# Row counts over pairs of columns, and ranks counted from 1024, in the dilation beside an attention

## The chip, the cores and the metric

The kernel runs on one core of a Trainium2 chip. The time is the device time of one execution in microseconds (us), as the median of several runs; lower is better. The engines are PE (TensorE, matrix products; its weight loads are listed as PEld), DVE (VectorE), ACT (ScalarE), POOL (GpSimd) and SP (SyncE, here a queue of DMAs). Each works through its own instructions in order, and they wait for one another by semaphores.

## What is computed

There are B = 16 graphs of N = 1024 nodes with D = 128 features, and an adjacency `adj` of floats, zero where there is no edge. Layer 0 is an attention with 8 heads over the edges, layer 1 a "dilation" of the adjacency and three SAGE layers on what it leaves:

```python
# layer 0
scores = q @ k.T / sqrt(HD); scores[adj == 0] = -inf
attn = softmax(scores) * adj;  attn = attn / (attn.sum(-1) + 1e-8);  x = x + (attn @ v) @ Wo.T + bo
# layer 1: dilation, row by row
def step(carry, n):
    row = carry[n]
    num = sum(row)
    sf = where(num > 10, (num + 1) // 2, 1)
    rank = cumsum(row)
    rm = row & (rank % sf == 0)          # only if mask[n] and num > 1
    carry[n] = row & ~rm
    carry[:, n] = carry[:, n] & ~rm      # later rows see the removal
# then three times: relu(normalise((adj_d @ h / deg) @ Wr + h @ Wx + b)), batch norm; a last product
```

The dilation needs the running count (rank) of every row's edges. A row with more than 10 edges loses the edges of rank sf and 2 sf.

## The kernel before

All instructions of PE, ACT and DVE stand in an order written out by hand: each engine executes in the order in which the Python code emits.

**Attention** (`attention`, L472 to L613). A *turn* is one graph b, one half c of the query nodes (512) and one of 8 blocks m of 128 key nodes; there are 256 turns. Each has two *half-steps*, g = 0 and 1, with four heads each: 512 half-steps. In a half-step PE writes the mask and the scores of the *next* half-step into PSUM (`scores`, L546 and L552), later the products with the values (`values`, L479 with v1 as the weights, L484 with the small eps8); ACT takes two exponentials of 128 x 1024 (L590); DVE multiplies both by the adjacency (L595). In half-step g = 0 PE also transposes a block of the adjacency (L497), and ACT copies it (L500) and makes the mask from it (L504). The preparation of the next graph (`prepare`: layer norm, projections to q, k, v) and the conclusion of the last one (`conclude`) are spread over the half-steps. `v1` holds the values of a graph, for each key block m and head h 16 columns of values, a column of ones (whose product gives the sum), and zeros up to 32; two such buffers take turns in one tile.

**Dilation** (`dilation`, L643 to L934) is a generator that `beside_attention` (L936) advances between the half-steps. It goes over 8 blocks k of 128 rows, all 16 graphs b together. Each block has two parts, called *stages* below:

- *Block stage*: the 128 x 128 diagonal block of each graph. `up` is the upper triangle of the edges (L741), `w` the running count in it by two scans (L747), restarted for each graph by a zero in `go_on`. The transposed edges (PE, L763) give `valid` (L779, L782); L785 makes of w the count plus 1024 where valid and 0 elsewhere. Seven rounds then find the removed edges: small instructions compute the rank that each row removes (L805 to L828), L830 compares w with it, and PE sums what is hit (L836 to L841). At the end (L845 to L858) the numbers needed for whole rows are formed: `mid_at`, `off` and `allof`.
- *Column stage*: the whole rows, graph after graph. For graph b, a scan on DVE (L893) counts along the 1024 columns; it adds the column before and the column itself, so that each value is the sum of two neighbouring counts. ACT takes the distance to the middle, |value - 3 num| by an Abs with a bias per row (L906). DVE compares it with `off` (L910: one comparison catches both ranks), and masks with the edges (L913, L915). PE transposes the result (L900), ACT copies it (L902), and DMAs write both to DRAM (L923 to L927). ACT then reads the rows of the next block as signs (L691, L695), and `survive` (L708) takes the edges out that earlier blocks removed.

`rk(b, lo, hi)` is a slice of the resident edges of the current 128 rows of graph b, as bf16 zeros and ones; columns 0 and 1 are zeros and the edges begin at column 2.

**The order.** Each `yield cost, when` of the dilation says what the coming work costs (in us, by hand) and in which half-step it may run: `when` 0 is at once, 1 the next half-step, "A" an even one (g = 0), "B" an odd one. The loop in `beside_attention` lets the dilation go on while `spent` is below a straight line from 0 to `total`, with 16 half-steps of lead. The steps with a scan yield "B" and those with the comparison yield "A", so that a graph takes two half-steps.

**After that** three SAGE layers run (L1204 on), bound to PE and DMAs; nothing of them is touched.

Of the kernel before, what the change touches and what calls it, by code (L numbers as in the profile page):

```python
# [10 lines left out]
F32 = mybir.dt.float32  # L11
BF = mybir.dt.bfloat16
F16 = mybir.dt.float16
U8 = mybir.dt.uint8
I32 = mybir.dt.int32
AF = mybir.ActivationFunctionType
ALU = mybir.AluOpType
# [4 lines left out]
P = 128  # L22
# [4 lines left out]
ROUNDS = 7  # L27
# [7 lines left out]
def swept(ctx: ExitStack, tc: tile.TileContext, t: dict, out: bass.AP, flag: bass.AP):  # L35
# [8 lines left out]
    nc = tc.nc  # L44
    x, adj, nodemask = t["x"], t["adj"], t["nodemask"]
    B, N, D = x.shape
    H = 8
    HD = D // H
    NB = N // P
    HB = NB // 2  # L50
    HN = N // 2
# [115 lines left out]
    def first_part(p1):  # L167
# [71 lines left out]
            )  # L239


        v1_both = shared.tile([P, 2, NB, H, 32], F32, name="v1_both", tag="aT2")
        v1s = [v1_both[:, i] for i in range(2)]
        for v1 in v1s:
            nc.vector.memset(v1[:, :, :, HD:], 0.0)
            nc.vector.memset(v1[:, :, :, HD : HD + 1], 1.0)
        never = one.tile([P, P], BF, name="never")
        nc.vector.tensor_scalar(never, ident, -BIG, None, ALU.mult)

# [35 lines left out]
        def prepare(b):  # L285


            yield False
            xt = xts.pop(b)
            h = shared.tile([P, NB, D], F32, name=f"h_{b}", tag="s", bufs=2)  # L290
            hT = shared.tile([P, N], F32, name=f"hT_{b}", tag="s", bufs=2)

            def turned(c, bank=(ps_m, "m")):
                pt = bank[0].tile([P, 512], F32, name=f"pt_{b}_{c}", tag=bank[1])
                for i in range(HB):
                    nc.tensor.transpose(pt[:, i * P : (i + 1) * P], h[:, c * HB + i, :], ident)
                yield "evict"
                nc.scalar.copy(hT[:, c * HN : (c + 1) * HN], pt[:, :HN])


            kT = pool.tile([P, N], F32, name=f"kT_{b}", tag="kT")

            def query(c, bank=(ps_m, "m")):
                pq = bank[0].tile([P, 512], F32, name=f"pq_{b}_{c}", tag=bank[1])
                nc.tensor.matmul(pq, wts["Wq"], hT[:, c * HN : (c + 1) * HN], start=True, stop=True)
                yield "evict"
                for g in range(2):
                    nc.scalar.activation(  # L308
                        qTs[c][:, g, :], pq, AF.Identity, bias=bq[:, g : g + 1], scale=own[:, g : g + 1]
                    )  # L310

            def key(c, bank=(ps_m, "m")):
                cc = slice(c * HN, (c + 1) * HN)
                pk = bank[0].tile([P, 512], F32, name=f"pk_{b}_{c}", tag=bank[1])
                nc.tensor.matmul(pk, wts["Wk"], hT[:, cc], start=True, stop=True)
                yield "evict"
                nc.scalar.activation(kT[:, cc], pk, AF.Identity, bias=bk)

            v1 = v1s[b % 2]

            def value(c, bank=(ps_m, "m")):
                pv = bank[0].tile([P, HB, D], F32, name=f"pv_{b}_{c}", tag=bank[1])
                start_with(pv, 0)
                for i in range(HB):
                    n = (c * HB + i) * P
                    nc.tensor.matmul(
                        pv[:, i, :], hT[:, n : n + P], wts["Wv"], start=False, stop=(i == HB - 1)
                    )
                yield "evict"
                nc.scalar.copy(  # L330
                    v1[:, c * HB : (c + 1) * HB, :, :HD], pv.rearrange("p k (h d) -> p k h d", d=HD)
                )

            if b == 0:

                first = layer_norm_relu(h, xt, "a0", 0, HB)
                for _ in range(2):
                    next(first)
                yield "weights"
                yield from first  # L340
                yield "weights"
                yield "biases"
                yield from turned(0)
                yield "turn 1"
                second = layer_norm_relu(h, xt, "a0", HB, NB)
                for _ in range(2):
                    next(second)
                yield from key(0)
                qTs = [pool.tile([P, 2, HN], F32, name=f"qT_{b}_0", tag="qT")]
                yield from query(0, (ps_d, "d"))  # L350
                yield from second
                ready[b] = (xt, qTs, kT, v1)
                yield True
                yield from value(0, (ps_d, "d"))
                yield True
                yield from turned(1)
            else:
                yield from layer_norm_relu(h, xt, f"a{b}")
                for c in range(2):
                    yield True  # L360
                    yield from turned(c)
                for what in (key, value):
                    yield True
                    yield from what(0)

                yield "half 1"
                qTs = [pool.tile([P, 2, HN], F32, name=f"qT_{b}_0", tag="qT")]
                yield True
                yield from query(0)

            ready[b] = (xt, qTs, kT, v1)
            for what in (key, value):
                yield True
                yield from what(1)
            yield "half 0"
            qTs.append(pool.tile([P, 2, HN], F32, name=f"qT_{b}_1", tag="qT"))
            yield True
            yield from query(1)
# [93 lines left out]
        def attention():  # L472
# [3 lines left out]
            def values(acc, v1, m, g, es, ws):  # L476

                for j in range(4):
                    nc.tensor.matmul(  # L479
                        acc[g][32 * j : 32 * j + 32, :], v1[:, m, 2 * j + g, :],  # L480
                        ws[j // 2][:, j % 2, :], start=(m == 0), stop=False,
                    )
                for j in range(4):
                    nc.tensor.matmul(  # L484
                        acc[g][32 * j : 32 * j + 32, :], eps8,
                        es[j // 2][:, j % 2, :], start=False, stop=(m == NB - 1),
                    )
# [141 lines left out]
        def each_half(ap):  # L629
            return ap.unsqueeze(1).to_broadcast([P, B // 2, P])  # L630
# [12 lines left out]
        def dilation():  # L643
# [9 lines left out]
            def rk(b, lo, hi):  # L653
                return rks[b // (B // 2)][:, b % (B // 2), lo:hi]
# [73 lines left out]
            for k in range(NB):  # L728
# [3 lines left out]
                dgs = [rks[i][:, :, 2 + n0 : 2 + n1] for i in range(2)]  # L732
                halves = [slice(0, B // 2), slice(B // 2, B)]

                up = shared.tile([P, B, P], BF, name=f"up_{k}", tag="mr", bufs=4)

                go_on = shared.tile([P, B, P], BF, name=f"go_on_{k}", tag="mr", bufs=4)
                nc.gpsimd.memset(go_on, 1.0)
                nc.gpsimd.memset(go_on[:, :, 0:1], 0.0)
                for dg, hb in zip(dgs, halves):  # L740
                    nc.vector.tensor_tensor(up[:, hb, :], dg, each_half(upto), ALU.mult)  # L741
                next(late, None)
                yield 1.3, 1
                w = shared.tile([P, B, P], F16, name=f"w_{k}", tag="mr", bufs=4)
# [15 lines left out]
                for c, hb in enumerate(halves):  # L760
# [1 line left out]
                    for b in range(B // 2):  # L762
                        nc.tensor.transpose(pd[:, b, :], dgs[c][:, b, :], ident_bf)  # L763
                    if c == 0:
                        nc.vector.tensor_copy(onw, w[:, :, P - 1])
                        for dg, of in zip(dgs, halves):
                            nc.vector.tensor_reduce(last1[:, of], dg, AX.X, ALU.add)
                    else:
# [13 lines left out]
                nc.vector.tensor_tensor(valid, valid, each(beyond), ALU.mult)  # L782
                yield 1.2, 1

                nc.vector.scalar_tensor_tensor(  # L785
                    w.rearrange("p b i -> p (b i)"), w.rearrange("p b i -> p (b i)"), 1024.0,
                    valid.rearrange("p b i -> p (b i)"), ALU.add, ALU.mult,
                )
                yield 2.3, 1
                final = shared.tile([P, B, P], BF, name=f"final_{k}", tag="mr", bufs=4)  # L790
                nc.vector.tensor_tensor(in_pairs(final), in_pairs(w), over_rows(end16), ALU.is_equal)
                yield 1.3, 1
# [49 lines left out]

                th = small.tile([P, 4, B], F32, name=f"th_{k}", tag="th", bufs=2)  # L845
                num, mid_at, off, allof = (th[:, i, :] for i in range(4))
                high = v[:, 3, :]
                nc.vector.tensor_tensor(mosts, most, gone[:, B : 2 * B], ALU.subtract)
                nc.vector.tensor_tensor(num, mosts, gone[:, :B], ALU.subtract)
# [3 lines left out]

                nc.vector.tensor_scalar(num, num, 0.5, 0.25, ALU.mult, ALU.add)
                nc.vector.tensor_scalar(num, num, MAGIC, MAGIC, ALU.add, ALU.subtract)
                nc.vector.tensor_scalar(mid_at, num, -3.0, 1024.0, ALU.mult, ALU.add)
                nc.vector.scalar_tensor_tensor(off, num, 1.0, high, ALU.add, ALU.mult)
                nc.vector.tensor_scalar(off, off, -1.0, None, ALU.add)  # L858
                yield 2.0, 1
# [29 lines left out]
                for i in range(B + 2):  # L889
                    b = i  # L890
                    if b < B:
                        wrs[b] = pool.tile([P, N], F16, name=f"wr_{k}_{b}", tag="wr", bufs=2)
                        nc.vector.tensor_tensor_scan(  # L893
                            wrs[b], rk(b, 1, N + 1), rk(b, 2, N + 2), -1023.0, ALU.add, ALU.add
                        )
                    b = i - 2
                    if 0 <= b:
# [2 lines left out]
                            nc.tensor.transpose(pe[:, j, :], ers[b][:, j * P : (j + 1) * P], ident_bf)  # L900
                        ets[b] = pool.tile([P, NB, P], BF, name=f"et_{k}_{b}", tag="et", bufs=2)
                        nc.scalar.copy(ets[b], pe)  # L902
                    yield (2.4 if i < B else 0.0), "B"
                    b = i
                    if b < B:
                        nc.scalar.activation(wrs[b], wrs[b], AF.Abs, bias=mid_at[:, b : b + 1])  # L906
                    b = i - 1
                    if 0 <= b < B:
                        er = ers[b] = pool.tile([P, N], BF, name=f"er_{k}_{b}", tag="er", bufs=3)
# [25 lines left out]

        def beside_attention():  # L936

            block = 1.3 + 4.6 + 3.9 + 1.4 + 1.2 + 3.6 + ROUNDS * 2.5 + 2.0 + 5.1 + 1.4 + B * 5.3 + 2.4
            total = B * 0.3 + NB * block
            n_att = 2 * B * 2 * NB  # L940
            todo = dilation()
# [1021 lines left out]
```

## Time and profile before

| What | Number |
|---|---|
| Time, median of 3 runs | 3443.05 us (3439.62 to 3444.79) |
| The profiled execution, its own time | 3445.77 us |
| Its span (first to last instruction) | 3443.9 us |
| Mean granted TensorE clock | 0.994 |
| PE busy over the span | 3364.4 us (98%) |
| DVE busy | 3096.0 us (90%) |
| ACT busy | 2287.3 us (66%) |
| POOL busy | 174.4 us (5%) |
| First exponential of the attention, end of the last | 20.4 us, 2355.9 us |
| First and last row scan (L893) | 177.5 us, 2307.4 us |

A line of the groups reads: line of the code, engine, operation, tile written <- tiles read, shape, count | busy us, mean ns of one | idle us of that engine just before, and who ended it. A line of the windows reads: window in us from the start of the span, its length, then busy us and count of instructions of PE, PEld, DVE, ACT and POOL, the granted clock, the busy share of the DMA engines and GB/s. A line of the timeline reads: start, time from the first start to the last end, engine, line, operation, tiles, shape, count. PE's busy time says little here, since its matrix products overlap and their ends are modelled; the distance from one start to the next says more.

### The profile page before, as it was taken

What the parts mean: (1) busy time and instruction counts of PE and PEld (TensorE: products, weight loads), DVE (VectorE), ACT (ScalarE), POOL (GpSimd) and SP (SyncE); (2) the same over time, 40 slices, a digit from 0 to 9 for tenths busy, and PEclk for the clock granted to TensorE, in tenths of its full rate; (3) what the DMA queues carried; (4) which work ended last, traced back from release to release, by engine and by line L of the source; (5) the groups of instructions that cost most, each with busy time, mean ns of one, the idle gap of its engine ahead of it and who ended that gap; (6) DMA issues with size and microseconds to landing.
All of it is one profiled execution on the core that took longest, in us unless ns stands there. A gap on an engine that the chain in (4) does not pass through costs nothing. (4 is left out here: it accounts for less than half of the span.)

```text
span 3443.9 us, 86074 instructions
## 1 busy us (share of the span) xinstructions
PE 3364.4 (98%) x34855; PEld 1882.4 (55%) x34855; DVE 3096.0 (90%) x5255; ACT 2287.3 (66%) x3781; POOL 174.4 (5%) x253
## 2 busy tenths in 40 slices
PE   8999999999999999999999999999999899999997
PEld 3333333333333333333334334336999899999997
DVE  7899999889989999998998999997888799988887
ACT  7699689779879869968876986884322344423234
POOL 2000000000000000000000000000000000000000
PEclk9999999999999999999999999999999999999999
DMA  7356457547637746745763773677999799989996
GB/s 238 107 171 197 137 148 200 153 129 222 187 117 213 213 124 182 227 142 157 228 191 121 229 236 120 185 218 248 345 334 337 271 354 353 350 309 350 356 352 222
DMA packets 650121, 772.27 MB, mean 224 GB/s; under 512 B 173264, under 2 KB 569168, under 8 KB 637424
## 3 DMA queue, kind: packets, MB, share of 16 engines
q1 hardware_dynamic: 632672, 708.58, 63.7%
q0 software_dynamic: 15456, 57.30, 4.9%
q8 instruction: 275, 4.51, 0.6%
q14 instruction: 134, 1.10, 0.1%
q10 hardware_dynamic: 1584, 0.79, 0.1%
HBM read 508.50 MB, written 157.29 MB: 193 GB/s over the span
## 5 line engine op out<-in xcount | busy, mean ns | idle before, releaser
L595 DVE TENSOR_TENSOR w<-e,aT 128x1024 f32<-128x1024 f32 x1024 | 1203.9, 1217 | 107.9 <-ACT e L590 107.4
L590 ACT ACTIVATE e<-sc 128x1024 f32<-128x1024 f32 x1024 | 990.4, 1020 | 341.7 <-PE sc L552 340.6
L1117 PE MATMUL pg<-y,aT 128*128 128x128 f32 (+1 forms) x6144 | 732.2, 275 | 0.0
L1117 PEld LDWEIGHTS pg<-y,aT 128*128 128x128 f32 x6144 | 710.3, 192 | 0.0
L479 PE MATMUL acc<-w,v_both 128*32 128x512 f32 x4096 | 637.2, 605 | 6.9 <-DVE w L595 3.8
L484 PE MATMUL acc<-e,eps 128*32 128x512 f32 x4096 | 617.3, 593 | 0.0
L552 PE MATMUL sc<-qT,kT 32*128 32x512 f32 x4096 | 584.3, 640 | 0.3 <-ACT qT L308 0.3
L146 DVE SCALAR_TENSOR_TENSOR aT<-mr,aT 128x1024 f32<-128x1024 bf16 x384 | 458.8, 1217 | 0.0
L484 PEld LDWEIGHTS acc<-e,eps 128*32 128x32 f32 x4096 | 159.1, 110 | 294.6 <-issue 286.0
L1140 ACT ACTIVATE sq<-o 128x512 f32<-128x512 f32 x96 | 60.6, 631 | 358.1 <-DVE o L1135 358.1
L893 DVE TENSOR_TENSOR_SCAN wr<-rk 128x1024 f16<-128x1024 bf16 x128 | 291.6, 2278 | 0.0
L546 PEld LDWEIGHTS <-never 32*32 32x32 bf16 x8192 | 79.1, 88 | 340.4 <-issue 317.6
L546 PE MATMUL sc<-nomask,never 32*32 32x512 bf16 x8192 | 249.2, 385 | 11.0 <-ACT e L590 7.5
L1158 ACT COPY hT<-pt 128x512 f32<-128x512 f32 x96 | 56.2, 585 | 267.7 <-PE pt L1154 259.3
L552 PEld LDWEIGHTS sc<-qT,kT 32*128 32x128 f32 x4096 | 160.1, 183 | 116.9 <-issue 116.1
L479 PEld LDWEIGHTS acc<-w,v_both 128*32 128x32 f32 x4096 | 100.7, 108 | 203.6 <-DVE w L595 105.0
L497 PEld LDWEIGHTS pa<-ident,a 128*128 128x128 f32 x1024 | 108.1, 141 | 181.7 <-issue 134.2
L906 ACT ACTIVATE wr<-wr,th 128x1024 f16<-128x1024 f16 x128 | 148.0, 1156 | 46.8 <-DVE wr L893 45.8
L497 PE MATMUL pa<-ident,a 128*128 128x128 f32 x1024 | 168.8, 288 | 6.8 <-DMA a<-in_adj 6.1
L504 ACT ACTIVATE nomask<-aT 128x512 bf16<-128x512 f32 x256 | 161.4, 630 | 8.1
L1135 DVE SCALAR_TENSOR_TENSOR o<-pg,rdeg,mine 128x128 f32<-128x128 f32 x384 | 108.1, 344 | 60.4 <-PE pg L1117 56.8
L500 ACT COPY aT<-pa 128x512 f32<-128x512 f32 x256 | 151.6, 592 | 4.7 <-PE pa L497 4.7
(226 smaller groups left out, 3844.5 us busy)
## 6 DMA issues: line engine op xcount, KB each, us to landing
aT<-aT_d SPq DMA_DIRECT2D x94, 2048.0 KB, 9.8
mr<-mr_d SPq DMA_DIRECT2D x188, 512.0 KB, 6.1
aT_d<-aT SPq DMA_DIRECT2D x256, 256.0 KB, 4.1
a<-in_adj SPq DMA_DIRECT2D x253, 256.0 KB, 4.1
ad<-in_adj SPq DMA_DIRECT2D x112, 512.0 KB, 4.2
nomask<-nomask SPq DMA_DIRECT2D x512, 96.0 KB, 2.7
nomask<-nomask SPq DMA_DIRECT2D x512, 64.0 KB, 2.7
nomask<-nomask SPq DMA_DIRECT2D x512, 32.0 KB, 2.8
```

Source lines behind the costliest of these rows:

```text
L146: nc.vector.scalar_tensor_tensor(part, mrs[h][:, j : j + 2, :].rearrange("p j n -> p (j n)"), 0.0, part, ALU.is_equal, ALU.mult)
L479: nc.tensor.matmul(acc[g][32 * j : 32 * j + 32, :], v1[:, m, 2 * j + g, :], ws[j // 2][:, j % 2, :], start=(m == 0), stop=False,)
L484: nc.tensor.matmul(acc[g][32 * j : 32 * j + 32, :], eps8, es[j // 2][:, j % 2, :], start=False, stop=(m == NB - 1),)
L497: nc.tensor.transpose(pa[:, k * P : (k + 1) * P], a[:, k, :], ident)
L500: nc.scalar.copy(aT[:, 0, :], pa)
L504: nc.scalar.activation(nomask[:, 0, :], aT[:, 0, :], AF.Relu, bias=1.0, scale=-1e38, accum_out=zeros[:, i : i + 1])
L546: nc.tensor.matmul(scs[j // 2][to : to + 32, j % 2, :], never[rows, rows], nomask[rows, j, :], start=True, stop=False, tile_position=(32 * ...
L552: nc.tensor.matmul(scs[j // 2][:, j % 2, :], kT[rows, mm], qTs[c][rows, g, :], start=False, stop=True, tile_position=(32 * j, 0),)
L590: nc.scalar.activation(e, scs[q], AF.Exp, scale=1.0 / math.sqrt(HD))
L595: nc.vector.tensor_tensor(w, es[q], aT.to_broadcast([P, 2, HN]), ALU.mult)
L893: nc.vector.tensor_tensor_scan(wrs[b], rk(b, 1, N + 1), rk(b, 2, N + 2), -1023.0, ALU.add, ALU.add)
L1117: nc.tensor.matmul(pg[:, i // 2, at : at + width], aT[:, j, i * P : (i + 1) * P], y[:, j, :width], start=(j == 0), stop=(j == NB - 1),)
```

## The change

1. *Counts over pairs of columns.* The scan takes columns 0, 2, 4, ... as one input and 1, 3, 5, ... as the other, and so makes 513 counts instead of 1024 values. They go into `pair_sums`, two buffers of 513 f16.
2. *Distances for even and odd columns apart.* Instead of one Abs over 1024 elements there are two over 512, with scale 2 and biases `at_even` and `at_odd`; each writes every other element of `wr`. One small threshold is added for it (`th` has five rows instead of four). `wr` is now taken at the Abs, no longer at the scan.
3. *Room for the pair sums.* `v1` holds 17 columns a head (values and the one) and 16 zeros at the end of a key block; the weights of L479 are still 32 columns, of which the upper 15 now belong to the following heads. The product's rows for them are not read. `pair_sums` lie behind the two v1 in the same tile.
4. *Ranks from 1024.* `up` becomes f16, and 1024 is added to its first column, so that the scan L747 counts from 1024. The multiplication with `valid` no longer adds 1024, and becomes a plain tensor_tensor; `onw` has 1024 subtracted.
5. *The hand-written costs* are lowered accordingly: 1.3 instead of 2.4 for the scan's step, 1.3 instead of 2.3 for the multiplication, and the sums of both in `block`.

```diff
-        v1_both = shared.tile([P, 2, NB, H, 32], F32, name="v1_both", tag="aT2")
-        v1s = [v1_both[:, i] for i in range(2)]
+        HW = HD + 1
+        VW = H * HW + 16
+        both = shared.tile([P, 4096], F32, name="both", tag="aT2")
+        v1s = [both[:, i * NB * VW : (i + 1) * NB * VW].rearrange("p (m w) -> p m w", w=VW) for i in range(2)]
         for v1 in v1s:
-            nc.vector.memset(v1[:, :, :, HD:], 0.0)
-            nc.vector.memset(v1[:, :, :, HD : HD + 1], 1.0)
+            nc.vector.memset(v1[:, :, H * HW :], 0.0)
+            nc.vector.memset(v1[:, :, HD : H * HW : HW], 1.0)
+        free = 2 * NB * VW
+        pair_sums = [
+            both[:, free + i * (HN // 2 + 1) : free + (i + 1) * (HN // 2 + 1)].bitcast(F16)[:, : HN + 1]
+            for i in range(2)
+        ]
...
                 nc.scalar.copy(
-                    v1[:, c * HB : (c + 1) * HB, :, :HD], pv.rearrange("p k (h d) -> p k h d", d=HD)
+                    v1[:, c * HB : (c + 1) * HB, : H * HW].rearrange("p k (h e) -> p k h e", e=HW)[:, :, :, :HD],
+                    pv.rearrange("p k (h d) -> p k h d", d=HD),
                 )
...
-                        acc[g][32 * j : 32 * j + 32, :], v1[:, m, 2 * j + g, :],
+                        acc[g][32 * j : 32 * j + 32, :], v1[:, m, (2 * j + g) * HW : (2 * j + g) * HW + 32],
...
-                up = shared.tile([P, B, P], BF, name=f"up_{k}", tag="mr", bufs=4)
+                up = shared.tile([P, B, P], F16, name=f"up_{k}", tag="mr", bufs=4)
...
                     nc.vector.tensor_tensor(up[:, hb, :], dg, each_half(upto), ALU.mult)
+                nc.vector.tensor_scalar(up[:, :, 0:1], up[:, :, 0:1], 1024.0, None, ALU.add)
...
-                        nc.vector.tensor_copy(onw, w[:, :, P - 1])
+                        nc.vector.tensor_scalar(onw, w[:, :, P - 1], 1024.0, None, ALU.subtract)
...
-                nc.vector.scalar_tensor_tensor(
-                    w.rearrange("p b i -> p (b i)"), w.rearrange("p b i -> p (b i)"), 1024.0,
-                    valid.rearrange("p b i -> p (b i)"), ALU.add, ALU.mult,
-                )
-                yield 2.3, 1
+                nc.vector.tensor_tensor(w, w, valid, ALU.mult)
+                yield 1.3, 1
...
-                th = small.tile([P, 4, B], F32, name=f"th_{k}", tag="th", bufs=2)
-                num, mid_at, off, allof = (th[:, i, :] for i in range(4))
+                th = small.tile([P, 5, B], F32, name=f"th_{k}", tag="th", bufs=2)
+                num, at_odd, off, allof, at_even = (th[:, i, :] for i in range(5))
...
-                nc.vector.tensor_scalar(mid_at, num, -3.0, 1024.0, ALU.mult, ALU.add)
+                nc.vector.tensor_scalar(at_odd, num, -3.0, None, ALU.mult)
+                nc.vector.tensor_scalar(at_even, num, -3.0, 2.0, ALU.mult, ALU.add)
...
                     if b < B:
-                        wrs[b] = pool.tile([P, N], F16, name=f"wr_{k}_{b}", tag="wr", bufs=2)
+                        row = rk(b, 0, N + 2)
                         nc.vector.tensor_tensor_scan(
-                            wrs[b], rk(b, 1, N + 1), rk(b, 2, N + 2), -1023.0, ALU.add, ALU.add
+                            pair_sums[b % 2], row[:, 0::2], row[:, 1::2], 0.0, ALU.add, ALU.add
                         )
...
-                    yield (2.4 if i < B else 0.0), "B"
+                    yield (1.3 if i < B else 0.0), "B"
                     b = i
                     if b < B:
-                        nc.scalar.activation(wrs[b], wrs[b], AF.Abs, bias=mid_at[:, b : b + 1])
+                        wrs[b] = pool.tile([P, N], F16, name=f"wr_{k}_{b}", tag="wr", bufs=2)
+                        for t, at in enumerate((at_even, at_odd)):
+                            nc.scalar.activation(
+                                wrs[b][:, t::2], pair_sums[b % 2][:, t : t + HN], AF.Abs,
+                                bias=at[:, b : b + 1], scale=2.0,
+                            )
...
-            block = 1.3 + 4.6 + 3.9 + 1.4 + 1.2 + 3.6 + ROUNDS * 2.5 + 2.0 + 5.1 + 1.4 + B * 5.3 + 2.4
+            block = 1.3 + 4.6 + 3.9 + 1.4 + 1.2 + 2.6 + ROUNDS * 2.5 + 2.0 + 5.1 + 1.4 + B * 4.2 + 2.4
```

## The prediction

> **What bounds the kernel now.** I read the page's busy shares and costliest groups first, then the busy time by window with one window per stage of the dilation, then the groups with their shapes apart, the waits, and the timeline of TensorE (PE).
>
> The two halves of the program differ. The change lies in the first, the attention with the dilation beside it (about 20 to 2356 us); the SAGE layers behind it keep their code. I cut the first part at the first and last row scan (L893) of each 128-row block: a "block stage" (ranks in the diagonal block, rounds) and a "column stage" (16 scans). Columns: window, its length, then busy time of PE, PEld, DVE, ACT, POOL.
>
> ```profile
> 177.50:315.80 138.30, 136.58 (x1464) 49.22 (x1464) 131.85 (x179) 133.51 (x219) 6.93 (x6) 1.00 0.63 182
> 453.10:593.40 140.30, 138.05 (x1452) 50.19 (x1455) 136.71 (x197) 133.35 (x219) 6.06 (x6) 1.00 0.65 186
> 736.30:878.20 141.90, 140.09 (x1472) 51.52 (x1464) 139.29 (x201) 134.60 (x219) 6.06 (x6) 1.00 0.67 196
> 878.20:1015.80 137.60, 136.63 (x1634) 51.28 (x1626) 123.98 (x219) 99.72 (x157) 7.85 (x8) 1.00 0.50 149
> 1015.80:1160.00 144.20, 142.18 (x1472) 51.59 (x1464) 141.63 (x201) 135.55 (x221) 6.06 (x6) 1.00 0.70 204
> 1299.20:1446.40 147.20, 144.76 (x1488) 52.16 (x1479) 144.04 (x201) 135.44 (x220) 6.06 (x6) 1.00 0.71 209
> 1585.90:1735.60 149.70, 147.10 (x1472) 52.12 (x1464) 145.95 (x200) 135.48 (x220) 6.06 (x6) 1.00 0.73 215
> 1876.70:2028.80 152.10, 148.98 (x1488) 50.94 (x1479) 148.97 (x202) 133.02 (x192) 6.03 (x6) 1.00 0.76 223
> 2169.50:2307.40 137.90, 135.91 (x1464) 48.34 (x1456) 135.52 (x159) 116.90 (x157) 7.57 (x10) 1.00 0.70 210
> ```
>
> The line at 878 is a block stage, the others are the eight column stages. In seven of those DVE is 97 to 98% busy; in the first, DVE is 95% and ACT 97%. ACT has 133 to 136 us of work in stages 0 to 6: it is second, 4 to 19 us behind the length of the stage. PE's own share must be taken from starts, since its ends are modelled:
>
> ```profile
> 1102.63 0.43 PE L546 MATMUL sc<-nomask,never 32*32 32x512 bf16 x16
> 1102.99 1.14 PE L552 MATMUL sc<-qT,kT 32*128 32x512 f32 x8
> 1104.07 0.66 PE L497 MATMUL pa<-ident,a 128*128 128x128 f32 x4
> ...
> 1115.79 1.06 PE L479 MATMUL acc<-w,v_both 128*32 128x512 f32 x8
> 1116.67 1.04 PE L484 MATMUL acc<-e,eps 128*32 128x512 f32 x8
> 1117.65 0.62 PE L900 MATMUL pe<-ident_bf,er 128*128 128x128 bf16 x8
> ```
>
> From start to start PE needs 0.36 (mask), 1.08 (scores), 0.88 (values) and 0.98 us (eps): 3.3 us a half-step (one turn of one g). A column stage has 31 half-steps (62 of L590): 102 us. Its 15 to 16 transposes of L497 (0.59) are 9 us, 16 of L900 (0.55) 9 us, projections, the context's transposes and biases about 13 us by their spacing: PE needs about 133 us, hardly less than ACT. A block stage needs about 132 of its 137 to 143 us: there PE bounds, and DVE idles 10% (124 of 137.6).
>
> **The change, part by part.** These rows price it:
>
> ```profile
> L595 DVE TENSOR_TENSOR w<-e,aT 128x1024 f32<-128x1024 f32 x1024 | 1203.9, 1217 | 107.9 <-ACT e L590 107.4
> L893 DVE TENSOR_TENSOR_SCAN wr<-rk 128x1024 f16<-128x1024 bf16 x128 | 291.6, 2278 | 0.0
> L906 ACT ACTIVATE wr<-wr,th 128x1024 f16<-128x1024 f16 x128 | 148.0, 1156 | 46.8 <-DVE wr L893 45.8
> ```
>
> ```profile
> L691 ACT ACTIVATE rk<-ad 128x1024 bf16<-128x1024 f32 x16 | 16.8, 1051 | 0.0
> L691 ACT ACTIVATE rk<-ad 128x512 bf16<-128x512 f32 x16 | 10.0, 626 | 0.0
> ```
>
> *Row scan, 128 times.* 1024 steps become 513. L595 does 1024 one-at-a-time elements in 1.217 us, the scan takes 2.278: about two such steps per element and some 0.15 us fixed. So 0.15 + 513 x 2.08 ns = 1.22 us; 1.06 us saved, 17.0 us of DVE per column stage, 136 in all. The inputs now have a step of two bf16 elements, which no row shows. [...]
>
> *Distances, 128 times.* One ACTIVATE of 1024 becomes two of 512. L691 gives (1051 - 626)/512 = 0.83 ns per element; L906's fixed part is 1156 - 850 = 306 ns, so a half takes about 0.73 us. Neighbouring ACTIVATEs overlap by 0.10 to 0.12 us in the timeline (L906 at 1113.62, the next at 1114.66), so the pair occupies 2 x 0.62 = 1.24 against 1.04: +0.20 us, 3.2 us per column stage, 26 in all. What waits behind them on ACT is the signs of the next block and then the exponentials of the next half-step, for which DVE and PE wait. The outputs have a step of two f16, shown by no row of ACT. Upper end: writes at half rate, each half as long as the old whole (1.156): +1.04 us. Lower end: no extra, were the fixed part hidden; the row's overlap excludes more than 0.12 of it. [...] I take +0.20.
>
> *Block stage.* w times valid: 2048 elements, 2.28 us (L785) to 1.21, as L791 (f16 in, 1.208) shows; adding 1024 to the first column and one more threshold are two small DVE instructions of 0.17 (L765's strided 16 elements); the replaced copy of onw costs the same. Net -0.73 us, 8 times. The f16/bf16 mix in L741, L779 and w times valid has no row; unpacked they would cost 0.54 each (32 times) and 1.07 (8). All of it lies on DVE in stages that PE bounds with 13 us of idle DVE: hidden. I put -2 us for all eight together, where DVE was the late one for a moment; if the cover fails, +26 at worst.
>
> *At no cost.* The new constants of the planner: I went through its loop with both sets, and the same step falls in the same half-step throughout, because the parity wish ends each, never the pace. v1 at 17 columns a head: the same count and width of weight loads, whose garbage columns are not read. The start: the cleared part of v1 shrinks (2 x 0.91 to about 2 x 0.2 us), but DVE then waits for x until 6.2 us anyway. pair_sums share a tile with v1: a wait by whole tile would tie scans to PE, but L330 fills one v half while PE reads the other with 0.0 idle. No DMA is added or moved. Of waits, the first Abs takes over from the scan the wait for a free wr buffer, and the scan waits for the Abs two columns back to free a pair_sums buffer; both partners ran a whole turn earlier, so nothing queues behind either.
>
> **Sum.** After the change DVE has 115 to 132 us per column stage, ACT 136.6 to 138.8 in stages 0 to 6, PE 133: ACT is next. DVE gets 97 to 98% of a stage that it bounds; I give ACT 97.5% (its 46 us of waits for the scan go, but PE is only 5 us behind). Stages 0 to 6 become 140.2, 140.0, 141.3, 142.3, 142.2, 142.2, 139.7: changes of +1.9, -0.3, -0.6, -1.9, -5.0, -7.5, -12.4. Stage 7, which reads no next block, has ACT at 120 and goes to PE's 131.5/0.98 = 134: -3.7. Together -29.5, with the block stages -31. On the profiled execution's 3445.77 us (span 3443.9, and 1.9 around it) that is 3414; on the median 3443.05, 2.7 lower, 3412. Of 142 us saved on DVE some 30 arrive.
>
> **Rivals.**
> - *ACT packs fully, or PE is next* (7%): stages 0 to 6 at ACT's bare sum, -50, stage 7 and block stages -12: 3381. For it: scores have over 1 us of lead before ACT needs them. Against: no engine in any stage is 100% busy.
> - *Three even engines, nothing left* (24%): stage 0 has DVE, ACT and PE level and gives the busiest only 96.5%. At 95.5 to 96.5% for ACT, stages 0 to 6 gain 5 to 15, in all -10 to -21, about 3427; a third of this chance is within 7 us of none. To the same result leads a change that does not do what it says, a strided scan that stays at 2.28.
> - *Slower: strided ACT writes* (12%). Place: the two Abs, in column stages already ACT's. At half rate ACT gets +16.6 us a stage: (941 + 116)/0.975 - 1014 = +70 for stages 0 to 6, 3507 with the rest. It decides from +0.47 us per pair, which is 0.87 us for a half instead of 0.73. [...]
> - *The forecast* (57%): 3400 to 3422.
>
> About 0.2% (7 us) is what a measurement of this kernel can tell from none. Faster 0.80 (the forecast, the first rival, two thirds of the second), same 0.08, slower 0.12. The range, 3386 to 3442, leaves out the slower case and the far end of the first.
>
> **What would show it.** Right: scan near 1.2 us, Abs halves near 0.73, column stages 0 to 6 all 139 to 143 us long with ACT at 97% and DVE at 82 to 94%, block stages unchanged, 31 half-steps in each. Wrong: a half over 0.87 us; a scan over 1.5; column stages that still grow from 138 to 152; ACT under 96% with waits for scores; block stages longer than now.

## The result, and the profile after

The changed kernel takes 3416.1 us (median of 4 runs, 3407.3 to 3420.0) where the kernel before, with a fourth run added, takes 3442.5 (3439.6 to 3444.8): a ratio of 0.9922, 95% interval 0.9903 to 0.9941. That is 26 us less (20 to 33 by the interval); 31 were forecast. The profiled execution took 3414.15 us, its span 3412.3.

Where the time went is best seen by pieces. From the first exponential of the attention to the end of the last it is 2309.3 us after (20.0 to 2329.3) and 2335.5 before: -26.2. The SAGE layers behind it took 1083.1 us in this profile and 1088.0 in that of before, and between 1083 and 1088 in the profiles of the experiments, whose code is the same there; those 5 us are not the change's. PE's instructions stand in the same order in both traces, but for neighbouring products with the values and with eps8, whose starts lie within one another; on ACT and DVE only those of the diff differ.

The windows after, cut at the first and last row scan of a block as before (columns: window, length, then busy time and count of PE, PEld, DVE, ACT, POOL); the line at 870 is the block stage before block 3, that at 1715 the one before block 6:

```profile
174.40:313.10 138.70, 134.25 (x1452) 49.09 (x1456) 116.32 (x178) 137.52 (x233) 4.86 (x6) 1.00 0.64 184
451.00:590.00 139.00, 134.16 (x1452) 49.11 (x1455) 121.40 (x196) 137.33 (x233) 4.99 (x6) 1.00 0.65 189
730.70:870.30 139.60, 134.54 (x1456) 49.22 (x1448) 124.15 (x200) 137.35 (x232) 5.00 (x6) 1.00 0.67 197
870.30:1010.10 139.80, 139.20 (x1639) 51.49 (x1642) 123.57 (x220) 102.10 (x160) 7.85 (x8) 1.00 0.50 150
1010.10:1150.20 140.10, 134.97 (x1454) 49.47 (x1447) 126.64 (x200) 138.06 (x233) 5.00 (x6) 1.00 0.71 208
1290.30:1431.50 141.20, 135.93 (x1460) 49.82 (x1456) 128.86 (x200) 138.61 (x234) 5.00 (x6) 1.00 0.71 208
1572.90:1715.10 142.20, 136.91 (x1455) 50.86 (x1448) 130.35 (x199) 138.68 (x234) 4.99 (x6) 1.00 0.75 217
1715.10:1862.20 147.10, 144.59 (x1798) 54.98 (x1798) 128.67 (x245) 102.20 (x160) 6.88 (x8) 0.99 0.48 146
1862.20:2003.30 141.10, 139.53 (x1464) 51.08 (x1460) 132.86 (x201) 136.02 (x205) 4.97 (x6) 1.00 0.77 229
2147.80:2280.10 132.30, 131.19 (x1452) 48.09 (x1448) 120.25 (x159) 121.07 (x170) 6.50 (x10) 1.00 0.72 216
```

Before, the column stages grew from 138 to 152 us with DVE, at 97 to 98% in seven of the eight. Now the first seven are all 139 to 142 us long; ACT is busy 96.5 to 99% of them, and DVE 84 to 94%. The bound has passed from DVE to ACT, as the experiments with added work below show.

With the shorter scan this cut has moved: the column stages hold 244.5 half-steps in all instead of 247.5. For comparisons of lengths, all kernels are therefore cut at the same exponentials from here on, namely at those that in the kernel before start first behind each edge of a stage. So cut, stage 6 and the sum of the stages 0 to 6, before and then after:

```profile
1877.20:2031.70 154.50, 151.38 (x1502) 52.18 (x1505) 151.34 (x203) 135.86 (x197) 6.03 (x6) 1.00 0.76 224
sum 1030.90, PE 1014.26 PEld 364.72 DVE 1004.95 ACT 959.35 POOL 43.26; mean PE 144.89 PEld 52.10 DVE 143.56 ACT 137.05 POOL 6.18
```

```profile
1862.80:2008.00 145.20, 143.63 (x1508) 52.52 (x1507) 136.76 (x206) 140.72 (x214) 4.97 (x6) 1.00 0.78 231
sum 1009.30, PE 977.69 PEld 358.52 DVE 904.69 ACT 994.04 POOL 34.80; mean PE 139.67 PEld 51.22 DVE 129.24 ACT 142.01 POOL 4.97
```

The stages 0 to 6 are 21.6 us shorter in sum, stage 7 is 4.2 shorter, the part behind it 0.8. The block stages, the first of them counted from the first exponential on, are 0.2 longer. In the seven column stages ACT has 34.7 us more to do, DVE 100 less.

The busy time of each engine over the span, and the groups that answer to those of before, from the page:

```profile
PE 3316.5 (97%) x34855; PEld 1870.2 (55%) x34855; DVE 2967.2 (87%) x5271; ACT 2328.2 (68%) x3909; POOL 163.8 (5%) x253
L603 DVE TENSOR_TENSOR w<-e,aT 128x1024 f32<-128x1024 f32 x1024 | 1206.1, 1219 | 193.3 <-ACT e L598 191.8
L915 ACT ACTIVATE wr<-both,th 128x512 f16<-128x512 f16 x256 | 205.1, 879 | 1.7 <-DVE both L900 1.5
L900 DVE TENSOR_TENSOR_SCAN both<-rk 128x513 f16<-128x513 bf16 x128 | 155.9, 1218 | 0.0
```

DVE's waits for the exponentials have gone from 107 to 192 us, ACT's waits for the scan from 46 to 2: the same exchange, seen from the waits. Over the whole span ACT's busy time has grown by 40.9 us (from 2287.3 to 2328.2), where 26 were forecast. The scan takes 1.218 us, as forecast; a half of the distances takes 0.879, not 0.73.

### The profile page after: what moved, and what is told of

Same layout as the page of the kernel before. It is cut to its first block, busy times and chain, and to the rows that moved or that the text cites. A ratio compares the mean times of both kernels' runs of the same rounds, so it can differ in the third digit from the quotient of the medians.

```text
span 3412.3 us, 86211 instructions
## 1 busy us (share of the span) xinstructions
PE 3316.5 (97%) x34855; PEld 1870.2 (55%) x34855; DVE 2967.2 (87%) x5271; ACT 2328.2 (68%) x3909; POOL 163.8 (5%) x253
## 5 line engine op out<-in xcount | busy, mean ns | idle before, releaser
L487 PE MATMUL acc<-w,both 128*32 128x512 f32 x4096 | 574.4, 605 | 5.8 <-DVE w L603 5.2
L492 PE MATMUL acc<-e,eps 128*32 128x512 f32 x4096 | 561.3, 593 | 0.0
L492 PEld LDWEIGHTS acc<-e,eps 128*32 128x32 f32 x4096 | 144.1, 110 | 299.7 <-issue 294.8
L554 PE MATMUL sc<-nomask,never 32*32 32x512 bf16 x8192 | 268.0, 384 | 35.1 <-ACT e L598 32.0
L554 PEld LDWEIGHTS <-never 32*32 32x32 bf16 x8192 | 87.3, 87 | 376.5 <-issue 354.1
L915 ACT ACTIVATE wr<-both,th 128x512 f16<-128x512 f16 x256 | 205.1, 879 | 1.7 <-DVE both L900 1.5
L487 PEld LDWEIGHTS acc<-w,both 128*32 128x32 f32 x4096 | 88.4, 108 | 150.4 <-issue 50.4
L900 DVE TENSOR_TENSOR_SCAN both<-rk 128x513 f16<-128x513 bf16 x128 | 155.9, 1218 | 0.0
```

What stands on the lines that cost most here:

```text
L487: nc.tensor.matmul(acc[g][32 * j : 32 * j + 32, :], v1[:, m, (2 * j + g) * HW : (2 * j + g) * HW + 32], ws[j // 2][:, j % 2, :], start=(m ...
L492: nc.tensor.matmul(acc[g][32 * j : 32 * j + 32, :], eps8, es[j // 2][:, j % 2, :], start=False, stop=(m == NB - 1),)
L554: nc.tensor.matmul(scs[j // 2][to : to + 32, j % 2, :], never[rows, rows], nomask[rows, j, :], start=True, stop=False, tile_position=(32 * ...
L900: nc.vector.tensor_tensor_scan(pair_sums[b % 2], row[:, 0::2], row[:, 1::2], 0.0, ALU.add, ALU.add)
L915: nc.scalar.activation(wrs[b][:, t::2], pair_sums[b % 2][:, t : t + HN], AF.Abs, bias=at[:, b : b + 1], scale=2.0,)
```

## The experiments

**What bounds now.** Two kernels add one useless instruction per graph to the column stages of the changed kernel, one on ACT and one on DVE, working in place on a spare piece of a tile, so that nothing waits for them.

```diff
                                 bias=at[:, b : b + 1], scale=2.0,
                             )
+                        nc.scalar.copy(idle_a, idle_a)          # the one on ACT, 128x448 bf16
...
                             pair_sums[b % 2], row[:, 0::2], row[:, 1::2], 0.0, ALU.add, ALU.add
                         )
+                        nc.vector.tensor_tensor(idle_v, idle_v, idle_v, ALU.mult)   # the one on DVE, 128x320 f32
```

On ACT:

> The changed kernel with one more ACT instruction per graph in the column stages, behind the Abs (128 x 448 bf16 in place, of no use, about 0.57 us long and 0.47 us of ACT). Theory (ACT sets the end of column stages 0 to 6 now): each gets about 7.5 us longer, stage 7 a little, 3416 + 50 to 58 = about 3468. Rival (PE or DVE sets it, ACT has room): at most +15, 3431.

Measured: 3453.8 us (ratio to before 1.003, 1.0021 to 1.0039), 38 more than the changed kernel. On DVE:

> The changed kernel with one more DVE instruction per graph in the column stages, behind the row scan (128 x 320 f32 in place, of no use, about 0.48 us: 7.7 us per stage, 61 in all). Theory (DVE is off the path in column stages 0 to 5): hidden there, 2 to 5 us in stage 6, so 3416 to 3424. Rival (DVE still bounds): all of it, +50 to +61, about 3470.

Measured: 3417.3 us (0.9926, 0.9909 to 0.9942), 1 more. Each added group, first of the kernel with more ACT work, then of that with more DVE work:

```profile
L921 ACT COPY both<-both 128x448 bf16<-128x448 bf16 x128 | 71.5, 558 | 0.0
```

```profile
L905 DVE TENSOR_TENSOR both<-both 128x320 f32<-128x320 f32 x128 | 59.7, 466 | 0.0
```

And their stages 0 and 3 in the windows, in the same order:

```profile
176.80:321.90 145.10, 136.00 (x1452) 49.72 (x1448) 116.22 (x181) 143.93 (x247) 4.86 (x6) 1.00 0.61 180
1030.50:1176.80 146.30, 136.28 (x1453) 49.65 (x1449) 126.73 (x200) 144.74 (x250) 4.99 (x6) 1.00 0.69 200
```

```profile
174.90:313.60 138.70, 134.38 (x1456) 49.53 (x1456) 121.85 (x195) 137.42 (x233) 4.86 (x6) 1.00 0.63 182
1011.30:1151.50 140.20, 135.49 (x1452) 49.33 (x1445) 131.94 (x215) 138.12 (x234) 5.00 (x6) 1.00 0.71 207
```

6.4 us more ACT work made stage 0 6.4 us longer, and 6.7 made stage 3 6.2 longer. 5.5 and 5.3 us more DVE work made them 0.0 and 0.1 longer. So ACT sets the length of these stages. The time grew by 38 us and not by the 50 to 58 expected, for two reasons. The column stages, cut at the same exponentials, grew by 45 us in sum: 6.1 to 6.9 in each of the first six, but 4.7 in stage 6 and 1.4 in stage 7. And the block stages came out 5.9 us shorter than the changed kernel's. In the same way the 1 us of the kernel with more DVE work is a balance: its column stages are 5.4 us longer in sum, 4.5 of them in stages 5 to 7, and its block stages 6.8 shorter. What makes the block stages differ is looked at below.

**The price of the halves.** Both Abs write densely, the even columns first, and the comparison on DVE reads them interleaved.

```diff
-                                wrs[b][:, t::2], pair_sums[b % 2][:, t : t + HN], AF.Abs,
+                                wrs[b][:, t * HN : (t + 1) * HN], pair_sums[b % 2][:, t : t + HN], AF.Abs,
...
-                            er, wrs.pop(b), off[:, b : b + 1], allof[:, b : b + 1], ALU.is_equal, ALU.max
+                            er.rearrange("p (i t) -> p i t", t=2), wrs.pop(b).rearrange("p (t i) -> p i t", t=2),
+                            off[:, b : b + 1], allof[:, b : b + 1], ALU.is_equal, ALU.max,
```

> The two Abs write dense halves (even columns, then odd) instead of every other element, and the comparison on DVE reads them interleaved. Theory (the step of two f16 in ACT's output costs the 0.15 us by which a half is longer than forecast): a half falls from 0.88 to about 0.73 us, ACT's work in a column stage from 138 to about 133 us, DVE's grows by 0.67 x 16 = 11 us; stages 0 to 3 lose 2 to 3 us each, stages 5 and 6 gain 2 to 5 where DVE gets to 141 to 144 us; in all 3410 to 3422. Rival (the 0.15 us comes from something else in the half, as the scale or the f16 input): halves stay at 0.88 us, and the time goes up to 3420 to 3435.

Measured: 3399.9 us (0.9873, 0.9856 to 0.9889), better than either side expected. Its groups, and its stages 0 and 3:

```profile
L915 ACT ACTIVATE wr<-both,th 128x512 f16<-128x512 f16 x256 | 172.2, 732 | 5.6 <-DVE both L900 5.4
L922 DVE TENSOR_SCALAR er<-wr,th 128x1024 bf16<-128x1024 f16 x128 | 102.8, 803 | 0.0
```

```profile
174.30:310.80 136.50, 133.60 (x1456) 49.02 (x1456) 119.82 (x180) 134.46 (x232) 4.86 (x6) 1.00 0.63 185
1004.20:1142.40 138.20, 134.59 (x1451) 49.22 (x1444) 129.82 (x200) 135.04 (x234) 5.26 (x6) 1.00 0.71 208
```

A half now takes 0.732 us: the step of two f16 in ACT's output had cost 0.147 us for 512 elements, and nothing else in the half did. From the start of the first half to that of ACT's next instruction it is now 1.23 us (median), where the prediction had 1.24. The comparison on DVE grew by 0.27 us (0.536 to 0.803) and not by the 0.67 expected; the column stages are 10.9 us shorter in sum. The rest of the gain lies in the block stages (8.0 us shorter in sum), which this edit does not touch; the next experiment is about them.

**A wait in the block stages.** In the changed kernel the block stages before blocks 6 and 7 are longer than before (143.7 us against 139.3, and 140.4 against 138.3, cut at the same exponentials), against the forecast. DVE's waits at its line on the removed edges, from 170 to 2330 us (columns: us in total, times, longest), before and after:

```profile
DVE rk L708 <- DMA gl<-mr_d: 2.9, 3, 1.8
```

```profile
DVE rk L716 <- DMA gl<-mr_d: 9.3, 5, 4.0
```

The timeline of the changed kernel at the longest (SPq is SP issuing a DMA), and the granted clock (the number before the last two) in windows around it:

```profile
1744.48 2.28 DVE L756 TENSOR_TENSOR_SCAN w<-go_on,up 128x1024 f16<-128x1024 bf16 x1
...
1745.70 0.32 SPq L710 DMA_DIRECT2D gl<-mr_d  x1
...
1750.76 0.96 DVE L716 SCALAR_TENSOR_TENSOR rk<-rk,gl 128x768 bf16<-128x768 bf16 x1 [4.00 <-DMA gl<-mr_d]
...
1751.64 2.36 DVE L603 TENSOR_TENSOR w<-e,aT 128x1024 f32<-128x1024 f32 x2
...
1752.92 0.14 PEld L487 LDWEIGHTS acc<-w,both 128*32 128x32 f32 x4 [2.55 <-DVE w L603]
```

```profile
1740.00:1752.00 12.00, 10.99 (x92) 3.17 (x88) 7.97 (x12) 8.24 (x11) 0.00 (x0) 1.00 0.78 236
1752.00:1758.00 6.00, 5.00 (x24) 1.24 (x24) 6.00 (x5) 0.69 (x2) 0.00 (x0) 0.72 0.57 172
```

`survive` of the last graph stands behind the first scan of the diagonal block. DVE got there, but the load of what was removed had only been issued at 1745.7 and landed 5 us later; the products of two exponentials stood behind it on DVE, PE waited for them, and in the 6 us from 1752 on its granted clock was 0.72. Moving these last two removals one scan back gives the load a half-step more:

```diff
                 nc.vector.tensor_scalar(up[:, :, 0:1], up[:, :, 0:1], 1024.0, None, ALU.add)
-                next(late, None)
                 yield 1.3, 1
```

> The changed kernel with the two removals that are left over for the next block stage (survive for the last two graphs) moved one step back each: behind the first and the second scan of the diagonal block instead of behind the triangle and the first scan. Theory (DVE gets there sooner now and waits for the load of the removed edges, 9.3 us in five waits, once with a drop of PE's clock): waits gone, -4 to -10, about 3409. Rival (these waits lie in PE's cover or are chance): within 3 us of the changed kernel's 3416.

Measured: 3410.7 us (0.9904, 0.9888 to 0.9921). The wait is gone from the profile, and the block stages are 6.1 us shorter in sum, while the column stages are 1.0 longer. That the wait goes is shown; that some 5 us come of it rests on one profile of each kernel, for the intervals of the two times overlap. The kernels with dense halves, with more DVE work and with more ACT work have 0.9, 3.2 and 3.4 us of this wait left instead of 9.3; their block stages are 8.0, 6.8 and 5.9 us shorter than the changed kernel's, though nothing in these stages was edited. So some of the wait is a matter of when DVE arrives. The two edits together:

> Dense halves and late removals together. Dense halves alone took 16 us, late removals alone 5. Theory (the dense kernel's block stages, 11 us shorter than the changed kernel's, had already lost most of the same wait for the load of the removed edges, by DVE coming later): not additive, 3396 to 3401. Rival (two independent gains): 3393 to 3395.

Measured: 3401.9 us (0.9891, 0.9874 to 0.9909): not additive, no better than dense halves alone, and 1 us above the range of the theory. Against late removals alone, where the wait is gone on both sides, the column stages are 10.0 us shorter and the block stages 1.2. So some 10 of the 16 us are what the profiles give to dense writes by themselves; the rest lies in the block stages, where less of the wait is left.

**The ranks alone.** The kernel before with only the ranks counted from 1024 (the diff's `up`, `onw` and the plain tensor_tensor).

> The kernel before with the ranks counted from 1024 alone (f16 triangle, 1024 added to its first column, a plain tensor_tensor with valid); scans and distances as before. Theory (block stages are bound by PE, the 0.7 us that DVE gains in each is hidden): 0 to -3, about 3441. Rival 1 (what DVE gains there arrives): -6. Rival 2 (the mix of f16 and bf16 is slow): the tensor_tensor instructions show over 1 us for 1024 elements, and the time is 3443 to 3450.

Measured: 3437.0 us (0.9987, 0.9978 to 0.9996), 3.9 us below its kernel before. In its profile the attention is 1.2 us shorter: the block stages by 1.5 in sum, while the column stages are 0.3 longer. So the profile shows -1, and the medians -4 with an interval of -1.4 to -7.6, which does not exclude the first rival's -6. The mixed types are not slow: the two of 1024 elements take 0.674 and 0.680 us, as in the kernel before, where the types were not mixed, 0.675 (L779) and 0.681 (L741). What the prediction calls unpacked is the price of f32, 1.217 us for 1024 elements (L595), 0.54 more. From its groups,

```profile
L780 DVE TENSOR_TENSOR valid<-pd,up 128x1024 bf16<-128x1024 bf16 x14 | 9.4, 674 | 0.0
L741 DVE TENSOR_TENSOR up<-rk,upto 128x1024 f16<-128x1024 bf16 x14 | 8.9, 680 | 0.0
L786 DVE TENSOR_TENSOR w<-w,valid 128x2048 f16<-128x2048 f16 x7 | 8.4, 1207 | 0.0
```

**What is next behind ACT.** The copy of the transposed marks (et) moves to DVE in blocks 0 to 2 of the changed kernel.

```diff
-                        nc.scalar.copy(ets[b], pe)
+                        (nc.vector.tensor_copy if k < 3 else nc.scalar.copy)(ets[b], pe)
```

> The changed kernel with the copy of the transposed marks (et, 128 x 1024 out of PSUM) on DVE instead of ACT in the blocks 0 to 2. ACT loses about 0.9 x 16 = 14 us in each of these column stages, DVE gains about 0.7 x 16 = 11. Theory (PE, at about 133 us, stands right behind ACT): these stages go from 139 to about 136 to 137 us, in all -5 to -9, about 3409. Rival (PE has more room than its starts show): they follow ACT down to DVE's 127 to 135, in all -15 to -30.

Measured: 3411.3 us (0.9919, 0.9904 to 0.9934). Its column stages 0 and 1:

```profile
175.20:310.20 135.00, 133.39 (x1452) 49.07 (x1448) 122.89 (x194) 126.86 (x219) 4.87 (x6) 1.00 0.64 186
448.40:585.10 136.70, 134.66 (x1450) 49.73 (x1445) 127.92 (x211) 125.99 (x218) 5.00 (x6) 1.00 0.64 188
```

ACT has 11 us less to do, the stages as windowed are 3.7, 2.3 and 2.7 us shorter, and neither ACT (92 to 94%) nor DVE (91 to 96%) fills them. PE, put at 133 us from its starts, is what is left; that it bounds is inferred, no run added work to it. The sum of the column stages falls by 8.9 us, but the block stages show 10.1 us of the wait for the load and are 3.9 longer. The same edit for two blocks upon dense halves and late removals:

> As the last, with the copy of the transposed marks on DVE in the blocks 0 and 1. Theory (ACT, DVE and PE stand within 3% of one another in column stages by then, PE at about 133 us): stages 0 and 1 go from 136.6 to about 135.5, in all -1 to -4. Rival (ACT still bounds alone): -10 to -20.

Measured: 3400.9 us (0.9884, 0.9869 to 0.9900), within 1 us of the last. In its stages 0 and 1 ACT is busy 92 and 90%, DVE 94 and 96%: again neither fills them. The lowest median is that of dense halves alone; no interval separates it from the last two.

## Why the prediction held, point by point

- *What bounds before, and what is next.* Right: DVE in column stages, ACT behind it. The two kernels with added work show that ACT now bounds and DVE no longer does. That PE stands behind ACT is inferred from the kernel with ACT's copy moved.
- *Row scan, -1.06 us 128 times.* Right to the third digit (1.218 for 1.22). The inputs' step of two, which no row of before shows, cost nothing here: the dense row's 0.15 us and 2.08 ns a step give 1.22, and the strided scan took 1.218.
- *Distances, +0.20 us per pair.* The size was wrong. A pair in the timeline after, and the instruction behind it:

```profile
1124.73 1.61 ACT L915 ACTIVATE wr<-both,th 128x512 f16<-128x512 f16 x2
1126.18 0.73 ACT L699 ACTIVATE rk<-ad 128x640 bf16<-128x640 f32 x1
```

From start to start the pair occupies 1.45 us against 1.05: +0.40. The missing 0.15 us per half is the strided write, which the trace of before could not show and for which the dense price was taken; that it would cost no more was the author's estimate. A half takes 0.879 us strided and 0.732 dense. So what the slower rival named, the strided write, was at work, though not at the half rate, which the prediction put at 1.156 us a half. The forecast's sign of being wrong, a half over 0.87 us, came true; in its sum, which breaks even at +0.47 per pair, 0.20 of the missing 0.27 were used up.
- *What a pair adds to ACT.* Yet ACT's work in stages 0 to 6 grew by 34.7 us, 0.31 per pair and not 0.40. In the trace of before, ACT instructions that start right behind another overlap it by 0.09 to 0.13 us, an Abs by 0.124 in the median; 62 of the 128 Abs started after an idle time there and had no such overlap, after the change 6 pairs of 128. That is worth about 0.05 us per pair, which the prediction had not counted; the rest of the difference the runs do not split.
- *ACT gets 97.5% of a stage.* Also off, the other way: 99% in stages 0 to 3, 96.5 to 98% in 4 to 6, 98.5% over all seven cut at the same exponentials. Put into the prediction's own sum, (959 + 35)/0.975 is 12.6 us more than with the 22.4 us it had for the pairs, and dividing by 0.985 instead takes 10 off again. Nothing in the prediction made these two errors meet: that the total came out so close is luck. That DVE's gain ends at ACT's work is not. Stage by stage the forecast was +1.9, -0.3, -0.6, -1.9, -5.0, -7.5, -12.4 and the measured change, cut at the same exponentials, +1.9, -1.5, 0.0, -2.2, -4.5, -6.0, -9.3; stage 7 has -4.2 for -3.7.
- *Block stages, -2 us.* They came out at +0.2. The ranks alone give -1.5 in their profile. What was missing is the wait for the load of the removed edges: with it gone, in the kernel with late removals, the block stages are 5.9 us shorter than before. The step "no DMA is added or moved" was true and not enough: DVE, with less to do, comes earlier to a load that is issued where it was. The profile of before had the wait already (2.9 us), and longer block stages, too, were named as a sign of being wrong.
- *Of 142 us some 30 arrive.* DVE's busy time over the span fell by 129 us (3096.0 to 2967.2); its durations, each counted in full, by 138 (3413.8 to 3275.7), since fewer neighbours overlap: 3787 of DVE's instructions start before the one ahead has ended, by 0.08 us in the median, where 3925 did. 26 arrived.

What stays open: how much of the wait for the load belongs to the change and how much to chance, since it is 2.9 us before, 4.8 with the ranks alone, and 0.9 to 10.1 in the kernels with paired scans whose removals stand where they were. Chance may enter the first block stage, too: before, the granted clock was 0.50 from 60.0 to 63.4 us, after it was 1.00 there, and the stage is 2.6 us shorter after. Without it the other block stages are 3.0 us longer than before.

## What to carry to other kernels

Cutting the work of the busiest engine was worth the distance to the next one and no more: sum each engine's work per stage, let the second stand at 96.5 to 99%, as it did here, and read the gain there. Cut both kernels at the same instruction when you compare stages. When an edit splits an instruction on that second engine, price its new access pattern from a row with that pattern, or measure it first: the dense version of the same halves gave another 16 us, some 10 of them in the stages where it acts. And look for DMAs that an engine, once it is faster, will reach before they land.

## What the runs showed of the hardware that was not expected

- An ACTIVATE of 128 x 512 f16 that writes every other element took 0.879 us, one that writes densely 0.732; in the changed kernel, where both halves write with the step, the one that starts to read at an odd element was no slower than the one that starts at an even element (medians 0.868 and 0.888).
- A tensor_scalar on DVE (f16 to bf16) took 0.536 us for 1024 elements in order, and 0.803 where its input alternates between two halves of a tile: 0.267 us more, 0.26 ns an element.
- A scan took 1.218 us for 513 elements and 2.278 for 1024: the difference is 2.07 ns an element, and 0.15 us are left over in both, though the shorter one reads with a step of two.
